# A graph network kernel whose head is issued in written order, with a product and the seen edges' sums moved

## The chip, the cores and the metric

The kernel runs on one core of one Trainium2 chip. The core has TensorE (PE), VectorE (DVE), ScalarE (ACT), GpSimd (POOL) and SyncE (SP), the last of which only issues DMAs here. The metric is the device time of one execution in microseconds, and the time of a kernel is the median of several executions. Everything is in float32 unless said otherwise.

## The reference

12500 nodes with 256 features, 200000 edges from `src` to `dst`, sorted by `dst`. Each edge has a weight.

```python
h = relu(layernorm(x))
e = h @ W_P + W_P_b + W_pos                       # 256 -> 128
for q, k, v, s, b in two_layers:                  # 8 heads of 16
    att = exp(clip(sum_per_head((e @ q)[src] * (e @ k)[dst]), -10, 10))
    att = att / (segment_sum(att, src)[src] + 1e-8)
    e = layernorm(segment_sum(att * (e @ v)[dst], src) + e) * s + b
x = x + e @ inv_w + inv_b                         # 128 -> 256
h = relu(layernorm(x))
out = x + segment_sum(edge_weight * (h @ w_nbr)[src], dst) + h @ w_own + bias
```

## The kernel before

Nodes are cut into 98 tiles of 128 (`NT`, the last one with 84 rows). Edges stand in columns of 128; gathers fetch one row per edge, 128 rows to a gather, from tables in HBM by indirect DMAs that POOL issues (L802).

**The head.** `sort_edges` sorts 256K packed keys by bitonic compares on DVE. A level has stages across columns (L543) and stages of its own (`stage`, L302 to L325: one minimum, L310, and one maximum, L312, each 128x1024), with `turned` (L327) transposing 128x128 blocks on PE and copying them back on ACT. There are 143 wide minima; 128 belong to the levels' `own` list, the others to the across parts and the last stage. `columns_out` writes the sorted columns. At the same time `embed` (L745 to L774) makes the embedding of a pair of tiles: statistics on DVE (L754, L755), the root on ACT (L758), scales on DVE (L759, L760), normalisation on ACT (L762), transposes on PE (L765), relu (L767), the product with `W_P` (L770, L771), a copy (L773), and `project`: transposes (L707), a copy (L709), the product with q, k and v (L718), copies (L719, L721) and stores to the table `tkv`. `plan_as_they_come` (L591) plans the third pass. The head's code (L1505 to L1543) writes these one after the other, and the framework's planner orders them by its costs. Two POOL memsets, of part of `q` and of all of `acc`, stand at the start. `general` is the flag that chooses between this short arm and a general one.

**Attention, layers 0 and 1** (`short_attention`, L1069). 163 steps of 8 gathered columns each ("far" edges). Their order is written out: the loop at L1265 to L1303 names what each engine does in a step, and works for nodes and for "seen" edges (edges whose other end is in the same or a neighbouring tile, handled without gathers) hang in slots, each with a step and a place in it (`put`, `other_work`). `seen(t, t0)` (L1085) registers a tile's loads at step t0 - 5, its main works at t0 - 3 to t0 - 1, and the addition at t0. `t0` is the step by which the tile's far edges are complete (`ends_by`). Then the node's after-works: `next_layer` (L972) in layer 0, `neighbour_rows` (L998) in layer 1. The latter ends with x + e @ inv_w (L1012, L1013), stored to `res_d`, a layernorm, transposes (L1042), a relu into `ht`, and `both` (L1047): two 512-wide products of `ht` with `w_nbr` and `w_own` side by side (L1051) plus the bias row (L1053). `rows` copies the first half for the store to the table `th`, and the own half into `q` and `acc` (L1059), which are the third pass's two accumulators (`acc1`).

**The third pass** (`short_neighbours`, L1306). 196 steps of 8 gathers from `th` (L802) into `kvg` (three buffers). In a step t: loads, `gathers(t + 2)` on POOL, `edge_hot(t + 1)` on DVE (L1343, ten selections into `hot`, two buffers), `adds(t - 1)` on DVE (L813), the results due, registers, and `sums(t)` on PE (L1356, L1358). `load_own` reads a tile's `res_d` three steps before its result; `result` (L1374) adds the accumulators to it and stores the output. The last step has three results due.

Of the kernel before, what the change touches and what calls it, by code (L numbers as in the profile page):

```python
# [37 lines left out]
P = 128  # L38
# [76 lines left out]
def gnn_kernel(ctx, tc, x, src, dst, edge_weight, wp_w, wp_b, w_pos, q1, k1, v1, ln1_s, ln1_b,  # L115
# [22 lines left out]
    bad = const.tile([P, 9], F32, name="bad")  # L138
# [61 lines left out]
    res_d = dram.tile([NT * P, GD], F32, name="res")  # L200
    place_d = dram.tile([P, W], BF16, name="place_d")
# [140 lines left out]
    def columns_out(pool, psum, a, b, c):  # L342
# [50 lines left out]
        fits = c[0:1, STEPS * (STEP + 2):STEPS * (STEP + 3)]  # L393
        nc.vector.tensor_tensor(fits, t8[:, STEP::STEP], firsts, op=OP.subtract)
        nc.vector.tensor_scalar(fits, fits, 1.0, None, op0=OP.is_gt)
        nc.vector.tensor_reduce(bad[0:1, 1:2], fits, AX.X, OP.max)
# [3 lines left out]
        nc.vector.tensor_tensor(bad[0:1, 1:2], bad[0:1, 1:2], fits[:, 0:1], op=OP.add)  # L400
# [29 lines left out]
    def sort_edges(pool, psum, mine, other, weight=None, idx=None):  # L430
# [87 lines left out]
        a, b = flipped(a, b, turn[:, 0:1])  # L518
        yield
        for level in range(1, LEVELS + 1):  # L520
            if level > LG and w is not None:
                bit = level - LG - 1
                a, b = flipped(a, b, turn[:, bit:bit + 1] if level == LEVELS else turn[:, 8 + bit:9 + bit])
                yield
                yield from turned(psum, a, b)
                a, b = b, a
                yield from turned(psum, w, w)
                for j in range(bit, -1, -1):
                    yield from stage(pool, a, b, w, LEVELS, j)
                    a, b = b, a  # L530
                yield from turned(psum, a, b)
                a, b = b, a
                yield from turned(psum, w, w)
            elif level > LG:
                yield from across(psum, a, b, level)
                if (level - LG) % 2:
                    a, b = b, a

                half = W // 4
                for c in (0, half):  # L540
                    lo, hi = (t[:, c:c + half] for t in (a, a[:, W // 2:]))
                    for op, t in ((OP.min, b), (OP.max, b[:, W // 2:])):
                        nc.vector.tensor_tensor(t[:, c:c + half], lo, hi, op=op)  # L543
                        yield
                a, b = b, a
            own = list(range(min(level, LG) - 1, -1, -1))
            if w is None:

                own = own[level > LG:len(own) - (level >= LG)]
            for j in own:  # L550
                yield from stage(pool, a, b, w, level, j)
                a, b = b, a
# [39 lines left out]
    def plan_as_they_come(pool, psum):  # L592
# [18 lines left out]
        room = pool.tile([P, NG, P], F32, name="room")  # L611
        nc.vector.tensor_tensor(room, d[:, :, 0:P], d[:, :, 1:], op=OP.is_gt)
# [17 lines left out]
        nc.scalar.copy(rows, pe[:NG])  # L630
        first, final = (rows[:, i, :].rearrange("g (w k) -> g w k", k=K) for i in range(2))
# [113 lines left out]
    def embed(node, psum, wp_sb, zb3, ones_b, q, tiles):  # L745

        n, many = rows_of(tiles[0]), len(tiles)
        mv = node.tile([P, 2, 2], F32, name="mv2", bufs=3)
        xts = []
        for i, t in enumerate(tiles):  # L750
            xt = node.tile([P, GD], F32, name="xt", bufs=5)
            nc.sync.dma_start(xt[:n], x[t * P:t * P + n, :])
            st = node.tile([P, 6], F32, name="st")
            nc.vector.bn_stats(st[:n], xt[:n])  # L754
            nc.vector.bn_aggr(mv[:n, i, :], st[:n])  # L755
            xts.append(xt)
        mean, dev = mv[:n, 0:many, 0], mv[:n, 0:many, 1]
        nc.scalar.activation(dev, dev, AF.Sqrt, bias=eps5[:n])  # L758
        nc.vector.reciprocal(dev, dev)  # L759
        nc.vector.scalar_tensor_tensor(mean, mean, -1.0, dev, op0=OP.mult, op1=OP.mult)  # L760
        for i, (t, xt) in enumerate(zip(tiles, xts)):
            nc.scalar.activation(xt[:n], xt[:n], AF.Identity, bias=mv[:n, i, 0:1], scale=mv[:n, i, 1:2])  # L762
            pt = psum.tile([P, 2, P], F32, name="pt", bufs=2)
            for k in range(2):
                nc.tensor.transpose(pt[:, k, :n], xt[:n, k * P:(k + 1) * P], ident[:n, :n])  # L765
            ht = node.tile([P, 2, P], F32, name="ht")
            nc.scalar.activation(ht[:, :, :n], pt[:, :, :n], AF.Relu)  # L767
            pz = psum.tile([P, 2 * GD], F32, name="pz")
            for k in range(2):
                nc.tensor.matmul(pz[:n, 0:D], ht[:, k, :n], wp_sb[:, k, :], start=(k == 0), stop=False)  # L770
            nc.tensor.matmul(pz[:n, 0:D], ones_b[:, :n], zb3, start=False, stop=True)  # L771
            e = node.tile([P, D], F32, name="e", bufs=4)
            nc.scalar.copy(e[:n], pz[:n, 0:D])  # L773
            project(node, psum, q, t, 0, e)  # L774
# [223 lines left out]
    def neighbour_rows(node, slots, weights, acc, acc1, t0, t):  # L998

        n = rows_of(t)  # L1000
        inv_sb, w2_sb = weights
# [42 lines left out]
        def relu():  # L1044
            ht = tiles["ht"] = node.tile([P, 2, P], F32, name="ht", bufs=1)
            nc.scalar.activation(ht[:, :, :n], tiles["pt2"][:, 0:2, :n], AF.Relu)

        def both():
            pz = tiles["pz"] = slots["psum"].tile([P, 4 * P], F32, name="out_c", tag="n2")
            for k in range(2):  # L1050
                nc.tensor.matmul(pz[:n], tiles["ht"][:, k, :n], w2_sb[:, k].rearrange("p a b -> p (a b)"),  # L1051
                                 start=(k == 0), stop=False)
            nc.tensor.matmul(pz[:n, GD:], ones_b[:, :n], rows3[:, 1, :], start=False, stop=True)  # L1053

        def rows():
            h = tiles["h"] = node.tile([P, GD], F32, name="out_rows")
            nc.scalar.copy(h[:n], tiles["pz"][:n, 0:GD])
            for h, to in enumerate(acc1):
                nc.scalar.copy(to[:n, t, :], tiles["pz"][:n, GD + h * D:GD + (h + 1) * D])  # L1059

        def store():
# [5 lines left out]
            (t3, "pe_out", both), (t3 + 1, "act_out", rows), (t3 + 1, "store", store))  # L1067

    def short_attention(wide, pool, psum, still, q, acc, layer, after, early=None):  # L1069
# [92 lines left out]
        before = -1  # L1162
        for t in range(NT):
            before = max(before + 1, (ends_by(t) - 1) // STEP + 1)
            seen(t, before)
# [140 lines left out]
    def short_neighbours(wide, pool, psum, acc1, plan):  # L1306
# [63 lines left out]
        def load_own(t):  # L1370
            xt = of["xt", t] = pool.tile([P, GD], F32, name="xt", bufs=6)
            nc.sync.dma_start(xt[:rows_of(t)], res_d[t * P:t * P + rows_of(t), :])

        def result(t):  # L1374
            n, xt = rows_of(t), of.pop(("xt", t))
            for h, to in enumerate(acc1):
                half = slice(h * D, (h + 1) * D)
                nc.vector.tensor_add(xt[:n, half], to[:n, t, :], xt[:n, half])
# [7 lines left out]
        for t in range(-4, steps + 1):  # L1386
            if t % 2 == 0:
                do(load, t // 2 + 2, steps // 2)
            for i in outs.get(t + 3 if t + 3 < steps else -1, ()):
                load_own(i)  # L1390
            if t == steps - 1:
                for i in outs[steps]:
                    load_own(i)
# [13 lines left out]
        for i in outs[steps]:  # L1407
            result(i)

    def short_arm(q, acc, acc1):  # L1410
        with tc.tile_pool(name="short", bufs=1) as wide, tc.tile_pool(name="short_p", bufs=1, space=PSUM) as psum, \
# [4 lines left out]
            with tc.tile_pool(name="short_a", bufs=1) as pool, tc.tile_pool(name="short_n", bufs=2) as node:  # L1416
                inv_sb = pool.tile([P, GD], F32, name="inv_sb")
                w2_sb = pool.tile([P, 2, 2, GD], F32, name="w2_sb")

                def load_weights():  # L1420
                    layer_rows(pool, True)
                    nc.sync.dma_start(inv_sb, inv_w)
                    for j, w in enumerate((w_nbr, w_own)):
                        nc.sync.dma_start(w2_sb[:, :, j, :], w.rearrange("(k p) n -> p k n", p=P))

                weights = (inv_sb, w2_sb)
# [4 lines left out]
            with tc.tile_pool(name="short_b", bufs=1) as pool:  # L1431
# [3 lines left out]
                short_neighbours(wide, pool, psum, acc1, plan)  # L1435
# [63 lines left out]
    nc.gpsimd.memset(acc.rearrange("p a b -> p (a b)"), 0.0)  # L1499
# [5 lines left out]
    with tc.tile_pool(name="sort_a", bufs=1) as sp, tc.tile_pool(name="node_a", bufs=2) as node, \  # L1505
            tc.tile_pool(name="come", bufs=1) as cp, tc.tile_pool(name="head", bufs=1) as hp, tc.tile_pool(name="spsum", bufs=2, space=PSUM) as spsum, \
            tc.tile_pool(name="npsum", bufs=1, space=PSUM) as npsum, \
            tc.tile_pool(name="cpsum", bufs=1, space=PSUM) as cpsum:
        for _ in sort_edges(sp, spsum, src, dst):
            pass  # L1510
# [5 lines left out]
        part = hp.tile([2, GD], BF16, name="part")  # L1516
        zb3 = hp.tile([3, D], BF16, name="zb3")
        row_of = lambda t: bass.AP(tensor=t.tensor, offset=t.offset, ap=[[0, 1], [1, t.shape[-1]]])
        nc.scalar.dma_start(left[0:1, 0:D], row_of(wp_b))
        nc.scalar.dma_start(left[0:1, D:], row_of(w_pos))  # L1520
        nc.vector.tensor_add(left[0:1, 0:D], left[0:1, 0:D], left[0:1, D:])
        for i in range(3):
            nc.vector.tensor_copy(part[0:1, 0:D], left[0:1, 0:D])
            nc.vector.tensor_sub(left[0:1, 0:D], left[0:1, 0:D], part[0:1, 0:D])
            nc.scalar.dma_start(zb3[i:i + 1], part[0:1, 0:D])
        for i, b in enumerate((inv_b, bias)):
            nc.scalar.dma_start(left[i:i + 1], row_of(b))
        for i in range(3):
            nc.vector.tensor_copy(part, left)
            nc.vector.tensor_sub(left, left, part)  # L1530
            for j in range(2):
                nc.scalar.dma_start(rows3[i:i + 1, j, :], part[j:j + 1])
        for t in range(0, NT - 2, 2):
            embed(node, npsum, wp_sb, zb3, ones_b, q, (t, t + 1))
        for t in range(NT - NT % 2 - 2, NT):
            embed(node, npsum, wp_sb, zb3, ones_b, q, (t,))
        for _ in plan_as_they_come(cp, cpsum):
            pass
        pb = cpsum.tile([P, 9], F32, name="pb", tag="turned")
# [40 lines left out]
```

## Time and profile before

| | us |
|---|---|
| median of 7 runs | 7353.97 (7348.05 to 7371.37) |
| profiled execution, its own time | 7359.23 |
| its span | 7357.4 |
| head: to the general flag / first layer work | 642.7 / 647 |
| layer 0, mean step | 12.89 |
| layer 1, mean step | 13.66 |
| third pass, from / mean step | 5089 / 11.5 |
| mean granted PE clock | 0.801 |

The profile is of one execution. Its span runs from the first to the last instruction on the core. Lines like `L310 DVE TENSOR_TENSOR keys<-keys 128x1024 f32<-128x1024 f32 x143 | 172.2, 1204 | 0.6` name a source line, engine, operation, the tiles written and read with partitions by elements, and how often; then busy us in all, mean ns of one, and idle us of the engine just ahead of them with what ended it. Lines with `<-` and three numbers are waits: us in total, times, the longest. "remote" stands for a releaser that the profile can't name, "issue" for time in which the engine waited for nothing that it shows. Shares of the chain of waits are shares of the time followed back from the end of a window.

### The profile page before, as it was taken

Reading aid. Unit: us, or ns where it says so; the run is one execution under the profiler, and the core shown is the slowest. Engines: PE = TensorE matmul, PEld = TensorE weight load, DVE = VectorE, ACT = ScalarE, POOL = GpSimd, SP = SyncE. Lnnn points to the kernel's source line nnn. Section 1 sums busy time; section 2 is a strip of 40 time slices with the busy share of each in tenths; the row PEclk is TensorE's granted clock in tenths of the full one; section 3 lists DMA queues with packets and bytes.
Section 4 is the critical chain, followed back from the end, with each engine's and each line's share of the span. In section 5 each row is a group of like instructions: output and inputs, shape, how many; then the busy total and the mean of one; then the engine's idle time right before and its main releaser. Section 6 shows DMA issues by size and latency. Waiting matters only on the chain.

```text
span 7357.4 us, 91646 instructions
## 1 busy us (share of the span) xinstructions
PE 4990.7 (68%) x26262; PEld 4121.1 (56%) x26262; DVE 4094.8 (56%) x9525; ACT 2690.1 (37%) x4814; POOL 3990.1 (54%) x4189
## 2 busy tenths in 40 slices
PE   6773777777776776777778777877555555555555
PEld 3443666666666665666666666664444444444444
DVE  8776666666666665666666666664333333333333
ACT  3442555555555554555555555553000000000000
POOL 0002555555555554555555555554666666666666
PEclk7666888888888887889988888888777777777777
DMA  3112444444444443444444444443333333333333
GB/s 97 57 58 75 125 130 128 129 126 130 129 128 128 131 124 114 130 129 128 128 133 128 126 134 127 127 130 98 90 95 97 97 101 104 102 107 110 107 113 111
DMA packets 536717, 839.01 MB, mean 114 GB/s; under 512 B 105934, under 2 KB 360093, under 8 KB 536235
## 3 DMA queue, kind: packets, MB, share of 16 engines
q0 software_dynamic: 200448, 547.62, 25.1%
q1 hardware_dynamic: 334617, 284.29, 13.6%
q8 instruction: 245, 4.01, 0.2%
q14 instruction: 237, 1.94, 0.1%
q10 hardware_dynamic: 1170, 1.15, 0.1%
HBM read 752.73 MB, written 79.91 MB: 113 GB/s over the span
## 4 chain that ended last, share of the span: by engine, by line
PE 35%; issue 16%; POOL 15%; DVE 15%; another core or an unknown queue 11%; ACT 4%; DMA 3%; DVEq 1%; SPq 0%; ACTq 0%; POOLq 0%
POOL kvg L802 15%; PE qe L1205 7%; PE ps L1244 6%; PE qe L1122 4%; DVE att L1217 3%; DMA kvg<-tkv,idx_a 2%; PE out_c L1051 2%; PE qe L1153 2%; DVE kvg L1215 2%; PE ps L1356 2%; PE pq L718 2%; PE qe L1207 1%; DVE hot L1343 1%; PE pz L770 1%
## 5 line engine op out<-in xcount | busy, mean ns | idle before, releaser
L802 POOL DMA_INDIRECT kvg<-tkv,idx_a x2608 | 2474.8, 949 | 2542.1 <-issue 1309.5
L802 POOL DMA_INDIRECT kvg<-th,idx_a x1568 | 1502.2, 958 | 813.7 <-issue 450.0
L1356 PE MATMUL ps<-kvg,hot 128*128 128x256 f32 x3136 | 1049.2, 483 | 981.6 <-issue 898.4
L1356 PEld LDWEIGHTS ps<-kvg,hot 128*128 128x128 f32 x3136 | 759.7, 248 | 1203.7 <-issue 1027.8
L1343 DVE TENSOR_SCALAR hot<-iota_f,place_a,plan 128x128 f32<-128x128 f32 x1960 | 521.4, 360 | 1433.8 <-remote 1245.4
L1244 PE MATMUL ps<-kvg,hot 128*128 128x136 f32 x5216 | 844.7, 309 | 347.4 <-issue 322.0
L1215 DVE TENSOR_TENSOR kvg<-qe,kvg 128x512 f32<-128x512 f32 x652 | 431.6, 687 | 1103.0 <-remote 373.7
L1244 PEld LDWEIGHTS ps<-kvg,hot 128*128 128x128 f32 x5216 | 750.2, 212 | 437.3 <-issue 377.6
L1205 PE MATMUL qe<-q,hot_t 128*128 x5216 | 845.6, 314 | 138.9 <-issue 42.1
L1205 PEld LDWEIGHTS qe<-q,hot_t 128*128 128x128 f32 x5216 | 768.2, 226 | 181.4 <-issue 77.4
L1122 PE MATMUL qe<-kvn,hot_s 128*128 128x128 f32 x4720 | 693.2, 299 | 93.4 <-issue 92.5
L1122 PEld LDWEIGHTS qe<-kvn,hot_s 128*128 128x128 f32 x4720 | 649.9, 215 | 106.4 <-issue 105.6
L1186 ACT ACTIVATE far<-spread,part_neg 128x1280 bf16<-128x1280 bf16 x326 | 446.4, 1369 | 19.6 <-DMA spread<-place_d 9.1
L1190 ACT ACTIVATE hot_t<-far,ones 128x1280 f32<-128x1280 bf16 x326 | 444.9, 1365 | 0.5
L1229 DVE TENSOR_TENSOR hot<-still,place_a 128x1152 f32<-128x1152 f32 x326 | 439.1, 1347 | 0.0
L1153 PE MATMUL qe<-rows_s,hot_e 128*128 128x136 f32 x1176 | 232.1, 346 | 299.4 <-DVE rows_s L1145 215.6
L1234 DVE TENSOR_TENSOR kvg<-still,kvg 128x1024 f32<-128x1024 f32 x326 | 394.9, 1211 | 22.6 <-ACT kvg L1223 16.2
L1217 DVE TENSOR_REDUCE att<-kvg 128x64 f32<-128x1024 f32 x326 | 397.7, 1220 | 11.2
L1153 PEld LDWEIGHTS qe<-rows_s,hot_e 128*128 128x128 f32 x1176 | 193.4, 238 | 341.5 <-issue 259.9
L813 DVE TENSOR_TENSOR acc<-acc,ps 128x256 f32 (+1 forms) x718 | 304.2, 424 | 122.1 <-PE ps L1246 49.0
L1102 ACT ACTIVATE far<-seen,part_neg 128x256 bf16<-128x256 bf16 (+1 forms) x588 | 337.8, 639 | 0.7
L1358 PE MATMUL ps<-kvg,hot 128*128 x784 | 296.6, 464 | 45.2 <-issue 44.2
(253 smaller groups left out, 6512.1 us busy)
## 6 DMA issues: line engine op xcount, KB each, us to landing
spread<-place_d SPq DMA_DIRECT2D x326, 256.0 KB
kvg<-tkv,idx_a POOLq DMA_INDIRECT x2608
kvg<-th,idx_a POOLq DMA_INDIRECT x1568
xt<-in_x_dram SPq DMA_DIRECT2D x194, 128.0 KB
spread<-ext_d SPq DMA_DIRECT2D x326, 64.0 KB
seen<-place_d SPq DMA_DIRECT2D x196, 96.0 KB
seen<-other SPq DMA_DIRECT2D x196, 96.0 KB
emb<-e SPq DMA_DIRECT2D x194, 64.0 KB
```

The costliest lines, as they stand in the source:

```text
L802: nc.gpsimd.indirect_dma_start(out=dest, out_offset=None, in_=table, in_offset=bass.IndirectOffsetOnAxis(ap=idx, axis=0))
L1122: nc.tensor.matmul(to[:, k, :], hot_t[:, at, :], kvn[:, b, half], start=(i == 0), stop=(i == len(have) - 1))
L1153: nc.tensor.matmul(out_of, its["hot"][:, k, :], its["rows"][:, k, :], start=(k == 0), stop=(k == SEEN - 1))
L1186: nc.scalar.activation(far, of.pop(("spread", i)), AF.Abs, bias=part_neg[:, 1:2])
L1190: nc.scalar.activation(hot_t.rearrange("p k e -> p (k e)"), of.pop(("far", i)), AF.Relu, bias=ones[:, 0:1], scale=-1.0)
L1205: nc.tensor.matmul(qe[:, k, :], hot_t[:, h * K + k, :], q[:, bass.ds(tiles[h * K + k], 1), :], start=(k == 0), stop=False)
L1215: nc.vector.tensor_mul(kk, qe, kk)
L1217: nc.vector.tensor_reduce(att, kvg[:, :, 0:D].rearrange("p k (h d) -> p k h d", d=HD), AX.X, OP.add)
L1229: nc.vector.tensor_tensor(hot, iota_p[:, None, :].to_broadcast([P, STEP + 1, P]), place_a[:, c:c + STEP + 1, None].to_broadcast([P, STEP + ...
L1244: nc.tensor.matmul(ps[:, bass.ds(at, 1), :].rearrange("p a b -> p (a b)") if k else ps[:, 0, :], of["hot", i][:, k, :], of["kvg", i][:, k, ...
L1343: nc.vector.tensor_scalar(hot[:, k, :], iota_f, plan[1][:, c:c + 1], plan[2][:, c:c + 1], op0=OP.is_equal, op1=OP.mult)
L1356: nc.tensor.matmul(ps[:, bass.ds(at, 1), :].rearrange("p a b -> p (a b)") if k else ps[:, 0, :], hot[:, w * K + k, :], hg[:, k, :], start= ...
```

## The change

It has three parts.

1. **The head in written order.** The framework's planner is switched off for the head. The sort yields after each minimum and each maximum of an `own` stage; after every second of these one slot of other work is issued. `embed` no longer issues anything itself; it returns nine works for a pair of tiles, which are given to the slots 3g - 3 (load), 3g, 3g + 1, ... 3g + 7 for the g-th group. There are 50 groups (48 pairs and the two last tiles), so slots run from -3 to 154. Seven slots are issued ahead of the compares, 128 within them, the rest after the sort. A pair has one load, one relu, one `e` copy and one store of `e`. The memset of `acc` moves behind the first own stage; the planning's pieces are issued every sixth slot from 30 on, the biases' at slots 20 and 40, with three `part` tiles for one. A minimum over a row of 1305 elements and a column of `bad` are added.

2. **The own-node product in the third pass.** In layer 1 `both` keeps only the product with `w_nbr` (two 256-wide matmuls); `ht` is stored to HBM (128 KB a tile), and `q` and `acc` are set to zero. In the third pass `load_own` reads `res_d` and `ht` four steps ahead, and a new `own(t)` on PE adds up `ht` @ `w_own`, `res_d`'s rows through the identity, and the bias row in PSUM, after the sums of the step before the result. `result` adds PSUM and accumulator.

3. **Seen edges three steps sooner.** Each tile's seen works hang three steps earlier than its far edges are complete (one tile to a step at most); the after-works stay.

```diff
@@ sort_edges
             for j in own:
-                yield from stage(pool, a, b, w, level, j)
+                for _ in stage(pool, a, b, w, level, j):
+                    yield "own"
                 a, b = b, a
@@ columns_out
+        nc.vector.tensor_scalar(t8, t8, float(NT), None, op0=OP.min)
...
@@ embed
+        def root():
+            nc.scalar.activation(of["dev"], of["dev"], AF.Sqrt, bias=eps5[:n])
+
+        def scales():
+            mean, dev = of["mean"], of["dev"]
+            nc.vector.reciprocal(dev, dev)
+            nc.vector.scalar_tensor_tensor(mean, mean, -1.0, dev, op0=OP.mult, op1=OP.mult)
...
+        def second():
+            et = node.tile([P, 2, P], F32, name="et", bufs=1)
+            nc.scalar.copy(et[:, 0:many, :n], of["pt"][:, 0:many, 0, :n])
+            of["pq"] = [psum.tile([P, 3 * D], F32, name="pq", bufs=2) for _ in tiles]
+            for i, pq in enumerate(of["pq"]):
+                nc.tensor.matmul(pq[:n], et[:, i, :n], qkv_sb[0].rearrange("p a b -> p (a b)"), start=True, stop=True)
...
+        return load, stats, root, scales, normal, first, embeds, second, results_of
@@ neighbour_rows
         def both():
+            nc.sync.dma_start(ht_d[t][:, :, :n], tiles["ht"][:, :, :n])
             pz = tiles["pz"] = slots["psum"].tile([P, 4 * P], F32, name="out_c", tag="n2")
             for k in range(2):
-                nc.tensor.matmul(pz[:n], tiles["ht"][:, k, :n], w2_sb[:, k].rearrange("p a b -> p (a b)"),
-                                 start=(k == 0), stop=False)
-            nc.tensor.matmul(pz[:n, GD:], ones_b[:, :n], rows3[:, 1, :], start=False, stop=True)
+                nc.tensor.matmul(pz[:n, 0:GD], tiles["ht"][:, k, :n], w_sb[:, k], start=(k == 0), stop=(k == 1))
...
-            for h, to in enumerate(acc1):
-                nc.scalar.copy(to[:n, t, :], tiles["pz"][:n, GD + h * D:GD + (h + 1) * D])
+        def nothing():
+            for to in acc1:
+                nc.vector.memset(to[:, t, :], 0.0)
@@ short_attention
-        before = -1
+        before, at = -1, 0
         for t in range(NT):
             before = max(before + 1, (ends_by(t) - 1) // STEP + 1)
-            seen(t, before)
+            at = max(at + 1, before - 3)
+            seen(t, at)
             after(slots, before, t)
@@ short_neighbours
+            ht = of["ht", t] = pool.tile([P, 2, P], F32, name="ht", bufs=7)
+            nc.sync.dma_start(ht[:, :, :n], ht_d[t][:, :, :n])
+
+        def own(t):
+            n, ht = rows_of(t), of.pop(("ht", t))
+            po = of["own", t] = psum.tile([P, 4 * P], F32, name="own", tag=f"n{1 + t % 2}")
+            for k in range(2):
+                nc.tensor.matmul(po[:n, 0:GD], ht[:, k, :n], own_sb[:, k], start=(k == 0), stop=False)
+            nc.tensor.matmul(po[:n, 0:GD], ident[:n, :n], of["xt", t][:n], start=False, stop=False)
+            nc.tensor.matmul(po[:n, 0:GD], ones_b[:, :n], rows3[:, 1, :], start=False, stop=True)
...
-                nc.vector.tensor_add(xt[:n, half], to[:n, t, :], xt[:n, half])
+                nc.vector.tensor_add(xt[:n, half], po[:n, half], to[:n, t, :])
...
             do(sums, t)
-        for i in outs[steps]:
+            for i in outs.get(t + 1, ())[:2]:
+                own(i)
+        for k, i in enumerate(outs[steps]):
             result(i)
+            for j in outs[steps][k + 2:k + 3]:
+                own(j)
@@ the head
-    nc.gpsimd.memset(acc.rearrange("p a b -> p (a b)"), 0.0)
...
-            tc.tile_pool(name="cpsum", bufs=1, space=PSUM) as cpsum:
-        for _ in sort_edges(sp, spsum, src, dst):
-            pass
+            tc.tile_pool(name="cpsum", bufs=1, space=PSUM) as cpsum, tc.manual_schedule():
...
+        when = (-3, 0, 1, 2, 3, 4, 5, 6, 7)
+        emit = {}
+        for g, tiles in enumerate(groups):
+            works = embed(node, npsum, wp_sb, zb3, ones_b, q, tiles)
+            for at, work in zip(when, works):
+                emit.setdefault(3 * g + at, []).append((-at, work))
...
+        own = 0
+        for kind in sort:
+            if kind == "own":
+                if own == 0:
+                    nc.gpsimd.memset(acc.rearrange("p a b -> p (a b)"), 0.0)
+                own += 1
+                if own % 2 == 0:
+                    next_slot()
+        while emit:
+            next_slot()
+        for _ in plan:
+            pass
```

## The prediction

> **What bounds the kernel now.** I read the engines and the granted clock of the whole, then 200 us windows inside each stage, then in each stage the waits, the chain of waits and the groups of instructions. Totals first: no engine is full, TensorE (PE) comes nearest.
>
> ```profile
> PE 4990.7 (68%) x26262; PEld 4121.1 (56%) x26262; DVE 4094.8 (56%) x9525; ACT 2690.1 (37%) x4814; POOL 3990.1 (54%) x4189
> PEclk7666888888888887889988888888777777777777
> ```
>
> Windows: length, then busy us of PE, PEld, DVE, ACT, POOL, then clock, DMA share, GB/s. They are one of the head (0 to 647), of attention layer 0 (to 2791), of layer 1 (to 5089) and of the third pass (to the end).
>
> ```profile
> 200.00:400.00 200.00, 143.71 (x448) 84.95 (x448) 156.74 (x291) 86.11 (x254) 0.00 (x0) 0.59 0.18 58
> 1400.00:1600.00 200.00, 146.49 (x957) 134.56 (x956) 127.63 (x253) 108.53 (x172) 117.65 (x124) 0.85 0.44 127
> 4000.00:4200.00 200.00, 155.06 (x974) 128.71 (x973) 126.57 (x260) 115.80 (x208) 111.79 (x119) 0.91 0.44 126
> 5600.00:5800.00 200.00, 111.53 (x361) 85.69 (x361) 73.31 (x260) 0.00 (x0) 134.58 (x141) 0.72 0.33 98
> ```
>
> The head is VectorE (DVE) with PE close behind at a clock of 0.59; the layers are PE with something else nearly as long; in the third pass PE has 88 of 200 us free.
>
> **1. The head.** Its waits and groups:
>
> ```profile
> DVE mv L759 <- ACT mv L758: 67.0, 30, 3.0
> L312 DVE TENSOR_TENSOR keys<-keys 128x1024 f32<-128x1024 f32 x143 | 174.0, 1217 | 0.0
> L310 DVE TENSOR_TENSOR keys<-keys 128x1024 f32<-128x1024 f32 x143 | 172.2, 1204 | 0.6
> L718 PE MATMUL pq<-qkv,et 128*128 128x384 f32 x194 | 141.4, 826 | 15.7 <-ACT et L709 14.8
> ```
>
> Compares run from 49.1 to 616.2, 567 us. In the timeline a wide stage (L310 and L312) repeats every 2.40 us, a 256-wide compare every 0.34, one of L501 every 0.40, of L543 every 0.65: 143 x 2.40 + 168 x 0.34 + 28 x 0.40 + 28 x 0.65 = 430 us. The embedding's seven DVE operations take 1.05 us a pair by pitch, 50 us in all. So 87 us are stalls, 67 of them L759 waiting for ACT's root, which the new order puts a slot later.
>
> After: a slot every wide stage outside the across levels, three slots a pair, 128 slots. DVE needs 3 x 2.40 + 1.05 = 8.25 us a pair. PE and ACT strictly in turn need, at this clock, about 9.7 (0.4 copy, 3.3 for L718's four, 1.1 transposes, 0.6 relu, 2.6 for the L770 and L771 matmuls, 0.4 copy, 0.9 transposes, 0.4 handing over); overlapped, 7.4 (143.7 us of PE over 19.5 pairs). I take 8.7, between the DVE bound and the chain in turn: 42.7 pairs x 8.7 = 371. The rest of the sort is 15 wide stages, the narrow ones, L501 and L543, 122 together, and 16 of the 41 us that they now wait for column turns (L310 28, L543 13): 138. The sort starts 6 us sooner (the cast behind the 11.3 us memset no longer delays it): 43 + 371 + 138 = 552; the memset beside the first compares and the extra minimum (a 1305-wide one took 0.82) add 3, the columns' way out 30 as now (616.6 to 642.8, with what follows to 647). But slots reach 131 of 154, so 6.3 pairs are computed only after that, with nothing to hide them: 54 us at 8.5. Sum 639 against 642.7, where the general flag is out: **-4**. At 8.25 a pair and 48 us of rest it is -29, at 9.7 and 61 it is +46.
>
> The memset of `acc` leaves a place where a cast lay in its shade: L1523 took 5.67 us there and 0.20 later, while an addition, L1521, took 0.28 in it. Moved, it stands beside compares with two SBUF inputs, the addition's kind, so about 1 us; the cast's case, a stop of 11, is the upper end. GPSIMD Engine Reference of the Trainium skill, section Key points, says that GpSimd contends on shared SBUF interfaces with DVE instructions in a 2-port mode or with two SBUF inputs. That speaks against the move, would make it up to 11 us instead of 1, and the row of the addition is against it.
>
> **2. Seen edges three steps sooner.** Same works, other meetings. About 1.8 tiles leave each layer's last three steps for its start; regressed on step times, a tile in a step adds 2.5 to 3.7 us. That is 4.5 to 6.7 a layer if the start has room: **-8** for both. One tile in five may meet other work, 20 x 1.2 = 24 a layer; bounds -40 and +40.
>
> **3. Own-node product out of layer 1.** Groups of 2900 to 4900 and the chain there:
>
> ```profile
> L1051 PE MATMUL out_c<-w_sb,ht 128*128 128x512 f32 x340 | 176.0, 624 | 18.3 <-issue 16.6
> L1053 PE MATMUL out_c<-rows,ones_b 3*128 3x256 bf16 x85 | 23.9, 281 | 4.5 <-issue 3.9
> L1012 PE MATMUL out_e<-inv_sb,et 128*128 128x256 f32 x174 | 63.1, 430 | 19.9 <-issue 19.8
> L1059 ACT COPY acc<-out_c 128x128 f32<-128x128 f32 x85 | 24.0, 283 | 0.0
> L1059 ACT COPY q<-out_c 128x128 f32<-128x128 f32 x85 | 23.1, 271 | 0.0
> by line: issue 14.5%; PE qe L1205 12.3%; PE ps L1244 12.2%; PE qe L1122 7.6%; PE out_c L1051 7.4%; DVE att L1217 3.9%; another core or an unknown queue 3.6%; PE qe L1153 3.3%; POOL kvg L802 3.3%; DVE kvg L1215 2.9%; PE qe L1207 2.8%; PE out
> ```
>
> PE loses half of L1051 and L1053: 88 + 23.9 = 112 us over 85 tiles, 129 over 98. 148 of L1051's 176 us (7.4% of 2000) lie on the chain, 0.84 of it: 129 x 0.84 = 108 is the most. How much other waits take back, layer 0 tells: its step is 12.89 us against 13.66, with 9.44 us of PE (146.49/200) against 10.59. Brought to one clock (x 0.85/0.91) layer 0 has 8.82, so 1.77 more PE made 0.77 more time, 0.43: 129 x 0.43 = 56. ACT's two copies, 54 us over 98 tiles, are mostly hidden at 115.80 of 200. I take **-60**, by layer 0, as it is the same loop; bounds -108 and 0. Added: two memsets of `acc` and `q` (L133's 128x128 one took 0.17 us, so 33 us over 98 tiles, DVE busy 63%) and a 128 KB store of `ht`. The store sits on SP's queue waiting for the relu, ahead of later `spread` and `seen` loads, which are issued steps early. **+2**; +33 if the memsets had no cover.
>
> TensorE: Matmul & The Clock Gate of the Trainium skill, section What's actually happening, has a clock of half speed after an idle window of about 3.4 us and full after a busy one. So taking PE work away can slow the rest. The rows agree in direction, 0.85 in layer 0 against 0.91. At 0.85 the 10.59 - 0.79 us of a step would grow by 0.7 and the gain be nearly gone; the factor from layer 0 already holds this loss.
>
> **4. Own-node product into the third pass.** There the gathers lead:
>
> ```profile
> L802 POOL DMA_INDIRECT kvg<-th,idx_a x1391 | 1332.9, 958 | 667.6 <-issue 400.3 <-remote 245.2 <-PE ps L1358 21.7
> L1356 PE MATMUL ps<-kvg,hot 128*128 128x256 f32 x2783 | 927.9, 482 | 862.3 <-issue 829.1 <-DMA kvg<-th,idx_a 24.4 <-DVE q L813 5.1
> DVE hot L1343 <- remote: 1091.4, 98, 17.2
> POOL kvg L802 <- remote: 245.2, 77, 4.6
> ```
>
> Eight gathers need 8 x (0.95 + 0.30) = 10.0 us; steps repeat as 12.4, 12.2, 10.0, mean 11.5. In the timeline POOL's late starts (6106.19, 6118.41) and DVE's (6105.96, 6118.18) come 0.8 us after the last landing of the step before (6105.2, 6117.4): sums end with the landings, then free the buffers. A tile adds six f32 instructions of 0.43 to 0.48 (L1012, L1356) and one bias row of 0.28: 3.0 us, 98 times, 295 us of PE, issued after a step's sums have freed the buffers. Next landings are 2.4 us off, and PE has some 5 us of the step free to catch up by the last. Its two loads go out four steps ahead on SP, behind the stores of results; own-to-result adds wait behind 3.6 us of `hot`. So nearly all is hidden: **+10**, bounds -20 (a clock above 0.72) and +200 (two of three steps wait: 65 x 3.0).
>
> **5. The end.** Tile 97's product waits for tile 95's result, then its own addition and store: **+2**.
>
> **Sum:** -4 - 8 - 60 + 2 + 10 + 2 = -58 on the profiled 7357.4 us span: 7299. That execution took 7359.2, 5.3 above the median of 7354.0, so a median near 7296.
>
> **Rivals.**
> A. *Larger gain:* DVE alone bounds the head (-29), layer 1 gives its chain share (-108), 3 to 5 as above: 7354 - 29 - 8 - 108 + 2 + 10 + 2 = 7223. For it: 0.84 of L1051 on the chain. Against: POOL waited 264.9 us there for PE's L1246 and 184.4 for L1042, waits that a free PE only moves. 0.12.
> B. *Slower by the third pass:* the release of `kvg` and `hot` comes behind the own product, so POOL starts late in each step with a tile. It decides once more than 0.7 us a tile shows, 68/98 of the gain elsewhere; 65 x 3.0 = 195 less 68 is 7481, half of it 7384. For: 245.2 us of POOL waits end with PE's sums. Against: own stands after the sums. 0.20.
> C. *Slower by the head:* PE and ACT in turn, 9.7 a pair, +46, and layer 1 only -20: 7354 + 46 - 8 - 20 + 14 = 7386. For: PE at half clock. Against: three pairs are in flight. 0.12.
> D. *Nothing comes of it:* gather and issue waits (14.5% of the chain) take layer 1's gain, the rest cancels: 7350. 0.08.
>
> My forecast has 0.48, alone 7240 to 7335. 0.2%, 15 us, is about what can be told from no change: faster 0.12 + 0.45 = 0.57, same 0.03 + 0.07 = 0.10, slower 0.33. The range, 7220 to 7450, leaves out the upper part of B and the low part of A.
>
> **What would show it.** Head: pairs every 8.3 to 9 us, L759's wait gone, 50 to 60 us of embedding after the last compare. Layer 1: steps of 13.3, L1051 at about 0.43 us each; clock below 0.9 would eat it. Third pass: steps still 11.5 with PE near 125 of 200 us; POOL kvg waits unchanged. Steps of 12.5 there, or a first gather after 660, make the prediction wrong.

## The result

| | us | ratio to before |
|---|---|---|
| before, 43 runs | 7358.1 (7337.35 to 7384.98) | |
| after, 17 runs | 7383.46 (7371.93 to 7399.6) | 1.0034, 95% interval 1.0026 to 1.0041 |
| after, the profiled execution | 7365.5 (span 7363.7) | |

The change makes the kernel 25 us slower; 58 us faster was forecast. The profiled execution was quicker than any of the 17 runs, so its stages account for 6 of the 25 us only; a second profile of the same kernel stands below.

One thing about the experiments first. They ran on six occasions, and the kernel before takes 7358, 7236 and 7224 us on three of them (granted clock 0.80, "slower chips" below) and 6050 to 6053 on the three others (0.89, "the faster chip"). These are names only: that it is the chip that differs is not shown, as the record numbers the chips of five occasions, and number 2 stands beside 6051 us and, 37 minutes later, beside 7224. Times are compared with the "before" of the same occasion; where stages of two occasions stand side by side, the text says so.

The profile after, engines and clock of the whole, then windows as shown of before (length, busy us of PE, PEld, DVE, ACT, POOL, clock, DMA share, GB/s):

```profile
PE 5008.7 (68%) x26850; PEld 4230.5 (57%) x26850; DVE 4127.4 (56%) x9721; ACT 2624.9 (36%) x4470; POOL 3976.1 (54%) x4189
PEclk7666888888888887899888888888777777777777
```

```profile
200.00:400.00 200.00, 137.00 (x495) 87.78 (x495) 191.55 (x335) 80.44 (x212) 0.00 (x0) 0.64 0.21 64
1400.00:1600.00 200.00, 141.28 (x931) 128.51 (x931) 128.28 (x259) 105.04 (x167) 116.58 (x124) 0.86 0.45 126
4000.00:4200.00 200.00, 146.89 (x945) 132.35 (x944) 124.92 (x276) 107.81 (x181) 108.03 (x114) 0.89 0.45 131
5600.00:5800.00 200.00, 110.49 (x381) 85.42 (x382) 73.35 (x260) 0.00 (x0) 134.06 (x142) 0.74 0.35 101
```

In the head DVE is now full, 191.55 of 200 us against 156.74. In layer 1 PE lost 8 us of 200, and the steps did not get shorter. The stages, taken from the traces (head: to the first L1217 reduction; layers: first to last of these; turns: what lies between two stages; third pass: first to last gather; end: from there):

| us | head | layer 0 | turn | layer 1 | turn | third pass | end |
|---|---|---|---|---|---|---|---|
| before | 683.7 | 2088.9 | 57.6 | 2213.3 | 51.4 | 2250.5 | 12.0 |
| after | 667.4 | 2094.6 | 61.5 | 2225.1 | 35.4 | 2256.2 | 23.5 |

The head gains 16 us, and the turn to the third pass 16 more; both layers, the third pass and the end each give some back. The groups of the head and, from 2900 to 4900, of layer 1 (count, busy us and mean ns, idle ahead):

```profile
L313 DVE TENSOR_TENSOR keys<-keys 128x1024 f32<-128x1024 f32 x143 | 174.1, 1218 | 0.0
L311 DVE TENSOR_TENSOR keys<-keys 128x1024 f32<-128x1024 f32 x143 | 173.6, 1214 | 2.2
L807 PE MATMUL pq<-qkv,et 128*128 128x384 f32 x194 | 134.6, 845 | 28.6 <-ACT et L804 28.6
```

```profile
L1094 PE MATMUL out_c<-w_sb,ht 128*128 128x256 f32 x340 | 94.2, 388 | 22.2 <-issue 21.8
L1102 DVE MEMSET q<- 128x128 f32 x85 | 14.0, 165 | 0.0
L1102 DVE MEMSET acc<- 128x128 f32 x85 | 14.0, 165 | 0.0
```

The product costs 94.2 us instead of 176.0 and 23.9, about as priced (88). Third pass, 5300 to 7300, groups and then the longest waits (us in total, times, longest):

```profile
L844 POOL DMA_INDIRECT kvg<-th,idx_a x1386 | 1315.8, 949 | 685.6 <-issue 393.3 <-remote 208.5 <-PE ps L1403 46.5
L1401 PE MATMUL ps<-kvg,hot 128*128 128x256 f32 x2768 | 857.0, 455 | 565.6 <-issue 456.8 <-DVE acc L855 53.5 <-DMA kvg<-th,idx_a 24.9
L1427 PE MATMUL own<-own_sb,ht 128*128 128x256 f32 x360 | 121.8, 461 | 33.6 <-issue 31.5 <-PE ps L1403 0.8
```

```profile
DVE hot L1388 <- remote: 945.1, 77, 14.8
POOL kvg L844 <- remote: 208.5, 66, 4.7
```

PE's idle time ahead of the first group of sums fell from 862 to 566 us, which is where the own products went; POOL's idle time is 686 against 668.

### The profile page after: what moved, and what is told of

It is laid out like the page before. It is cut to its first block, busy times and chain, and to the rows that moved or that the text cites. A ratio compares the mean times of both kernels' runs of the same rounds, so it can differ in the third digit from the quotient of the medians.

```text
span 7363.7 us, 92808 instructions
## 1 busy us (share of the span) xinstructions
PE 5008.7 (68%) x26850; PEld 4230.5 (57%) x26850; DVE 4127.4 (56%) x9721; ACT 2624.9 (36%) x4470; POOL 3976.1 (54%) x4189
## 5 line engine op out<-in xcount | busy, mean ns | idle before, releaser
L1401 PE MATMUL ps<-kvg,hot 128*128 128x256 f32 x3136 | 980.8, 458 | 669.6 <-issue 531.7
L1401 PEld LDWEIGHTS ps<-kvg,hot 128*128 128x128 f32 x3136 | 707.7, 232 | 880.0 <-issue 690.1
L1289 PE MATMUL ps<-kvg,hot 128*128 128x136 f32 x5216 | 880.9, 316 | 390.9 <-issue 367.3
L1289 PEld LDWEIGHTS ps<-kvg,hot 128*128 128x128 f32 x5216 | 783.7, 219 | 496.4 <-issue 441.7
L1151 ACT ACTIVATE hot_s<-far,ones 128x1280 f32<-128x1280 bf16 x196 | 267.2, 1363 | 233.0 <-remote 112.9
```

Source lines behind the costliest of these rows:

```text
L1289: nc.tensor.matmul(ps[:, bass.ds(at, 1), :].rearrange("p a b -> p (a b)") if k else ps[:, 0, :], of["hot", i][:, k, :], of["kvg", i][:, k, ...
L1401: nc.tensor.matmul(ps[:, bass.ds(at, 1), :].rearrange("p a b -> p (a b)") if k else ps[:, 0, :], hot[:, w * K + k, :], hg[:, k, :], start= ...
```

## The experiments

### The parts one by one, on a slower chip

Each is the kernel before with one part of the diff: the head; `at = max(at + 1, before - 3)` for the seen edges; the product moved; and head and product together.

> The kernel before with the head's part of the change alone. In the traces of before and after the first far gather goes out at 660.1 and 641.2 us of trace time, and the pairs of the embedding follow each other every 8.3 us. Both theories expect the head's gain to stay: 15 to 20 us less than before (7338 to 7343 against 7358), layers and third pass as before. If head work was only moved, the gain is gone by the end and the time is that of before within 5 us.

> The kernel before with the seen edges three steps sooner and nothing else. Theory A (the shift of the seen edges costs time in both layers, and hides in layer 1 what the moved product gains): 10 to 30 us slower than before, both layers longer. Theory B (layer 1 isn't set by PE, so that taking the product out gains nothing): within 5 us of before.

> The kernel before with the own-node product in the third pass and nothing else. Theory A: layer 1 gets 30 to 60 us shorter than its 2213, the third pass with its end some 15 us longer, so 15 to 45 us faster than before. Theory B: layer 1 within 10 us of 2213, the third pass and its end 15 to 20 us longer, so 5 to 30 us slower than before.

> The whole change without the shift of the seen edges. Theory A: 30 to 65 us faster than before, the sum of head and product. Theory B: the head's 15 to 20 us less and the product's 5 to 30 more, within 15 us of before. If the parts act on each other (a head that ends otherwise sets the layers' rhythm), the sum of the single parts misses this by over 10 us.

| before 7235.74 | median us | ratio, 95% |
|---|---|---|
| head | 7222.41 | 0.9978 (0.9969 to 0.9986) |
| seen edges three sooner | 7307.85 | 1.0096 (1.0080 to 1.0111) |
| product moved | 7217.96 | 0.9973 (0.9963 to 0.9984) |
| head and product | 7198.24 | 0.9941 (0.9925 to 0.9957) |

Theory A holds in its main point: the seen edges' shift alone costs 72 us, more than the other two gain, and more than the 10 to 30 that A expected. The single parts add up to +41 (-13 - 18 + 72); head and product together gain 38. Theory B falls, but A's 30 to 60 us from layer 1 were a little too many:

| us | head | layer 0 | turn | layer 1 | turn | third pass | end |
|---|---|---|---|---|---|---|---|
| head | 667.6 | 2044.9 | 58.2 | 2172.9 | 46.8 | 2231.0 | 13.8 |
| seen three sooner | 678.3 | 2062.9 | 62.2 | 2216.9 | 47.1 | 2231.9 | 13.7 |
| product moved | 677.0 | 2030.9 | 55.0 | 2145.3 | 38.5 | 2240.9 | 20.9 |
| head and product | 666.1 | 2035.4 | 55.4 | 2150.3 | 40.7 | 2240.2 | 22.8 |

The first row leaves layers and third pass as before, so it serves as their measure here. Each row is one profile: layer 0, which the moved product doesn't touch, is 14 us shorter in its row than in the first, so a layer's time is known to some 15 us only. The shift costs 18 us in layer 0, 4 at the turn and 44 in layer 1. The moved product gives 28 in layer 1 and 8 at the turn after it (46.8 to 38.5), and takes 10 in the third pass and 7 at the end: 19 in sum, beside the 18 of the medians.

### Why the shift costs

A tile comes about every five thirds of a step, so the seen works and a tile's first after-works repeat about every five steps. Theory M: seen works and after-works of tiles fall into the same step or not, depending on the shift modulo five. Theory N: being sooner is what costs. Shifts of two and of five, next to the kernel before again:

```diff
-            seen(t, before)
+            at = max(at + 1, before - 2)
+            seen(t, at)
```

> The kernel before itself, for a profile of it on the chip that runs the others of this call. Its stages, not its total, are wanted: layers near 2045 and 2173 us if the chip is like that of the runs with single parts, near 2089 and 2213 if it is like that of the first profile.

> The kernel before with the seen edges two steps sooner instead of three. Tiles come three to five steps. Counted by step modulo five, the seen edges' main PE work of a tile falls into a step with a tile's whole-row after-works in two of three tiles now, in three of three at a shift of three, in one of three at a shift of two. Theory M (what counts is which works meet in a step): not slower than before, 20 to 60 us faster. Theory N (being sooner is what costs, by longer lives of buffers or a crowded start): two thirds of the 72 us that three steps cost, 40 to 55 us slower.

> The kernel before with the seen edges five steps sooner, one whole period, so that the same works meet as before. Theory M: within 12 us of before. Theory N: 100 us slower or more.

They ran on the faster chip, and so shifts of two and three, and the whole change with a shift of two, were later put side by side, which came to the faster chip again:

> The kernel before with the seen edges two steps sooner. On a chip of the slower kind (kernel before above 7200 us): theory M (works that meet in a step) 20 to 70 us faster than before, theory N (being sooner costs) 40 to 55 us slower. On one of the faster kind (6050 us): 26 us faster, as in its first run.

> The kernel before with the seen edges three steps sooner, beside the shift of two on one chip. Slower kind of chip: 72 us slower than before, as in its first run, 90 to 140 above the shift of two by theory M, 20 to 30 by N. Faster kind: 25 to 50 us slower than before by M, 20 or less by N; the whole change there lost 45 us to the same change with a shift of two.

> The whole change with a shift of two. Slower kind of chip: by M the parts' sum, 13 + 18 us of head and product and 20 to 70 of the shift, so 50 to 100 us faster than before, where the whole change is 25 slower; by N 0 to 20 us slower. Faster kind: 95 us faster, as in its first run.

| faster chip, shift of | ratio, 95% | layer 1, mean step | turn after layer 0 |
|---|---|---|---|
| none (before 6050.4) | 1 | 10.52 | 38.2 |
| two | 0.9958 (0.9944 to 0.9971) | 10.27 | 48.4 |
| two again | 0.9964 (0.9951 to 0.9976) | 10.25 | 48.1 |
| three | 1.0078 (1.0063 to 1.0094) | 10.64 | 49.3 |
| five | 1.0049 (1.0035 to 1.0062) | 10.52 | 49.0 |

N falls: two steps sooner is faster, three slower, five has the steps of none. M holds for the steps and missed for five (28 us slower, 12 at most was expected; for three it was 53, with 25 to 50 expected): on this chip every shift makes the start of a layer longer, some 10 us at the turn and 8 to 22 ahead of layer 0 (660.2 without a shift, 667.9 to 681.7 with one; three more profiles with the same head and no shift have 653.5 to 664.3). That the first tiles' works now crowd the first steps is the likely reason, but no run singles it out. On the slower chip above, the start costs less: 4 us at the turn and 1 ahead of layer 0 (677.0 and 678.3). The whole change with a shift of two took 5957.79, 0.9849 (0.9835 to 0.9863).

What meets: layer 1's mean step by step number modulo five, steps 12 to 154, on the slower chips (the first two rows on one occasion, the whole change on another).

| step modulo 5 | 0 | 1 | 2 | 3 | 4 |
|---|---|---|---|---|---|
| no shift (head alone) | 13.44 | 13.26 | 13.89 | 13.25 | 13.63 |
| three (seen alone) | 13.37 | 13.80 | 13.08 | 13.66 | 14.97 |
| three (whole change) | 13.43 | 13.34 | 13.21 | 13.11 | 14.58 |
| two (whole change) | 13.94 | 13.21 | 13.17 | 13.26 | 12.90 |

With three, one step in five mostly holds a tile's main seen work, another's sums and a tile's whole-row after-works (counted from the loop, 19 of the 29 steps at 4; no step does with no shift or with two), and takes 14.6 to 15.0 us; the lighter steps don't give it back. PE is busy 12.55 us in these steps with the seen edges' shift alone, 10.94 with the head alone. 1.34 us more in some 32 steps make 43 of layer 1's 44 us.

On the faster chip other steps are the long ones, and what fits their times is the meeting of main seen work and whole-row after-works alone. Steps of layer 1 in which these two meet, by the same count, and the mean step there:

| step modulo 5 | 1 | 3 | 4 |
|---|---|---|---|
| no shift | 26 of 28, 11.69 | 7 of 29, 11.00 | 22 of 29, 10.94 |
| two | 7, 10.86 | none, 10.35 | 20, 10.85 |
| three | 28, 11.63 | 26, 11.98 | 21, 10.62 |

Down each column the time follows the count. The sums beside them, which mark the long steps on the slower chip (at 4), cost nothing here. So the steps' times follow the meetings on both, but which meeting costs most differs.

### Why layer 1 gained half of what was forecast

The product left out, with nothing in its place (no store of `ht`, no memsets), first by itself, then beside the moved one and the whole change:

```diff
-                nc.tensor.matmul(pz[:n], tiles["ht"][:, k, :n], w2_sb[:, k].rearrange("p a b -> p (a b)"),
-                                 start=(k == 0), stop=False)
-            nc.tensor.matmul(pz[:n, GD:], ones_b[:, :n], rows3[:, 1, :], start=False, stop=True)
+                nc.tensor.matmul(pz[:n, 0:GD], tiles["ht"][:, k, :n], w2_sb[:, k, 0], start=(k == 0), stop=(k == 1))
...
-            for h, to in enumerate(acc1):
-                nc.scalar.copy(to[:n, t, :], tiles["pz"][:n, GD + h * D:GD + (h + 1) * D])
```

> The kernel before without the own-node product in layer 1 and with nothing in its place: no store of ht, no memsets, the third pass as before (its sums start from what layer 1 left in q and acc, and the output lacks h @ w_own + bias). Layer 1 lost 28 us in the profile with the product moved. If the added store and memsets took back the rest, layer 1 is now 55 to 65 us shorter. If PE's work was worth only that much, because the clock falls as PE gets idle, layer 1 is 20 to 35 us shorter and the granted clock in it is 0.87 again, against 0.90.

> The whole change once more, for a profile on the chip of this call; the chips of the calls so far differ (the kernel before took 7358, 7236 and 6053 us on them). On a chip like the first two (granted clock 0.80): 15 to 45 us slower than before. On one like the third (0.89, where the layers' steps of 10.0 us are the eight gathers'): layer 0 within 10 us, layer 1 20 to 60 us shorter, the third pass 0 to 10 longer, so 10 to 60 us faster.

> The whole change with the seen edges two steps sooner instead of three. Theory M (works that meet in a step): 50 to 100 us less than the whole change at a clock of 0.80, 20 to 50 less at 0.89, and faster than before on either. Theory N: at most 25 us less than the whole change.

> The kernel before with the own-node product moved and nothing else, beside the one without that product. Third pass 5 to 12 us longer than before, its end 6 to 10. If the store of ht and the memsets cost the layers nothing, layer 1 is as short as in the kernel without the product, within 10 us; if they take back what was missing from the forecast, 25 us or more longer than that.

> Without the own-node product in layer 1 and with nothing in its place, third pass as before (the output lacks h @ w_own + bias and its sums start from what layer 1 left). At a clock of 0.80: layer 1 30 us shorter if PE's work is worth 28 us as in the profile with the product moved, 60 us if store and memsets took the rest. At 0.89: 80 us shorter, as in the first run of it.

| faster chip | ratio, 95% | layer 0 | layer 1 | third pass | end |
|---|---|---|---|---|---|
| before (6051.35; stages of the 6050.4 profile above) | 1 | 1620.4 | 1703.5 | 1967.2 | 13.2 |
| product left out, first time (beside 6053.19) | 0.9851 (0.9836 to 0.9866) | 1619.9 | 1620.0 | 1965.9 | 13.0 |
| product left out | 0.9843 (0.9830 to 0.9857) | 1621.5 | 1621.5 | 1965.3 | 12.8 |
| product moved | 0.9856 (0.9841 to 0.9872) | 1621.6 | 1623.2 | 1965.5 | 16.3 |
| whole change | 0.9916 (0.9903 to 0.9930) | 1626.8 | 1645.7 | 1968.3 | 17.3 |
| whole change, shift of two | 0.9843 (0.9830 to 0.9857) | 1617.2 | 1613.4 | 1964.3 | 17.0 |

Here layer 1 gains 80 us, until its step is 10.0 us, the eight gathers'; the first such run had been expected at 65 at most. Store and memsets cost no more than 2 us (1623.2 against 1621.5). In the third pass the moved product costs nothing, where 5 to 12 were expected, and 3 at the end. The whole change is 50 us **faster** on this chip. The last runs came to a slower chip (before 7224.34):

> The whole change with a shift of two, beside the whole change. On a chip of the slower kind (kernel before above 7200 us): 50 to 100 us faster than before if the parts add up there (13 + 18 + 20 to 70), within 20 us of before if the shift of two gains nothing there. On the faster kind: 95 us faster, as twice before.

> The whole change. Slower kind of chip: 15 to 45 us slower than before, so 70 to 130 above the shift of two. Faster kind: 50 us faster than before, 45 above the shift of two.

> Without the own-node product in layer 1 and with nothing in its place (the output lacks h @ w_own + bias and the third pass's sums start from what layer 1 left). Slower kind of chip: 25 to 45 us faster than before, with a lower clock and longer pauses ahead of PE's sums in layer 1, if it is PE's freed time that is given back there; 70 us or more if store and memsets took it. Faster kind: 95 us faster, as twice before.

| slower chip | median us | ratio, 95% | layer 0 | layer 1 |
|---|---|---|---|---|
| whole change, shift of two | 7200.62 | 0.9964 (0.9951 to 0.9977) | 2026.7 | 2144.0 |
| whole change | 7254.05 | 1.0041 (1.0028 to 1.0054) | 2044.5 | 2177.4 |
| product left out | 7199.60 | 0.9963 (0.9950 to 0.9976) | 2028.0 | 2149.9 |

The whole change is 30 us slower again, and 53 above its shift of two, where 70 to 130 were expected. M expected the shift of two to gain 20 to 70 us there by itself; 24 us of gain in all (17 to 35), where head and product alone reached 38 (31 to 54) on another occasion, say that it gains nothing. Whether it costs some 14 us stays open, as head and product alone did not run beside it. So on a slower chip a shift of two costs little or nothing and one of three costs much; that two helps is shown on the faster chip only. With the product left out and nothing added, the kernel is 25 us faster than its own before, and layer 1 only 23 us shorter than the 2172.9 of the head alone on the earlier occasion: the rest is given back by PE itself. Two views show it, head alone against product moved (same chip, 2900 to 4900): the window, and the group of the far edges' sums.

```profile
2900.00:4900.00 2000.00, 1606.51 (x9943) 1360.65 (x9942) 1267.98 (x2626) 1170.85 (x2062) 1119.05 (x1184) 0.90 0.46 132
```

```profile
L1285 PE MATMUL ps<-kvg,hot 128*128 128x136 f32 x2368 | 398.1, 316 | 148.4 <-issue 138.2 <-DMA kvg<-tkv,idx_a 8.9
```

Product moved:

```profile
2900.00:4900.00 2000.00, 1554.34 (x10012) 1410.04 (x10011) 1294.40 (x2839) 1157.62 (x1913) 1131.40 (x1197) 0.87 0.49 139
```

```profile
L1246 PE MATMUL ps<-kvg,hot 128*128 128x136 f32 x2400 | 419.3, 320 | 199.9 <-issue 185.6 <-DMA kvg<-tkv,idx_a 9.9 <-DVE hot_e L1138 1.2
```

By step (13.41 and 13.24 us): PE is busy 10.77 and 10.29 us, 0.48 less where 112 us over 85 tiles, 0.79 a step, were taken out; the clock fell from 0.90 to 0.87, and 10.0 us at 0.90 make 10.3 at 0.87. The pauses ahead of the sums grew from 1.00 to 1.32 us. So 0.79 taken out, less 0.31 and less 0.32, leaves 0.16, the 0.17 measured. The fit is closer than two profiles allow: their layer 0, which is the same code, differs by 0.08 us a step. The clock is the steadier part, 0.89 to 0.90 in the three profiles from slower chips that have the product in layer 1 and 0.87 to 0.88 in the six that don't; the pauses are 0.86 to 1.00 us a step with it and 0.96 to 1.32 without. On the faster chip the clock stays where it was, 0.97 with the product and 0.96 to 0.97 without (2400 to 3900).

## Why the prediction was wrong

- **Seen edges, -8 with bounds of 40 to either side: the step that failed.** Measured +72 alone, 80 us off and the largest miss of the sum; 53 from three to two within the whole change. The prediction spread the meetings evenly, "one tile in five", 1.2 us each; in fact the works repeat about every five steps, and a shift of three puts three of them into one, 1.34 us more in every fifth step of layer 1 and none of it given back elsewhere. It also counted on room at the layers' start, and the start got longer (the turn from 58.2 to 62.2 us). Its 2.5 to 3.7 us for a tile in a step is an estimate that no view here shows. No rival named this: both slower ones lay elsewhere.
- **Layer 1, -60: mechanism right, size off.** -28 on a slower chip, -80 on the faster one. The factor 0.43 from layer 0 stood at 28/129 = 0.22 where it was measured. TensorE: Matmul & The Clock Gate of the Trainium skill, section What's actually happening, has the clock halved after an idle window, and the fall from 0.90 to 0.87 agrees in direction; the prediction took the loss as held in its factor. The longer pauses it had not priced at all.
- **Third pass, +10: right,** 10 us on a slower chip (2231.0 to 2240.9), none on the faster one. The waits of POOL that rival B rests on went from 245.2 to 208.5 us and steps stayed at 11.5, so it is refuted; PE, from 5300 to 7100, went from 109 to 120 of 200 us, where near 125 was forecast. The turn ahead of it, 8 us shorter with the product moved, had no term.
- **The end, +2: 7 us** (13.8 to 20.9). After the last sums, at 7355.0 in the profile after, PE makes three tiles' products one by one until 7360.5, not one:

```profile
7355.41 1.03 PE L1427 MATMUL own<-own_sb,ht 128*128 128x256 f32 x4
7357.01 1.13 PE L1427 MATMUL own<-own_sb,ht 128*128 128x256 f32 x4
7358.71 1.09 PE L1427 MATMUL own<-own_sb,ht 128*84 128x256 f32 x4
```

- **The head, -4: -13,** within its bounds. Pairs follow every 8.3 us, the DVE bound and not 8.7; L759's successor, L774, waits 1.3 us among the compares, so the wait of 67.0 is gone there, and 40.1 us in the pairs after the sort, which nothing hides (the lines below: up to 565 us, then to 660). The columns' way out takes 27 us (542.6 to 569.2 in the timeline; 30 in the sum), and the pairs left over follow it and take 54 as forecast (570.6 to 624.2). What the sum had too long is the compares, which end at 542.6 and not at 555. Rival C is refuted.

```profile
DVE mv L774 <- ACT mv L770: 1.3, 4, 0.5
```

```profile
DVE mv L774 <- ACT mv L770: 40.1, 6, 7.6
```

- **The memset beside the compares costs nothing:**

```profile
43.55 11.33 POOL L1627 MEMSET acc<- 128x13464 f32 x1 [41.36 <-DVE keys L516]
```

```profile
45.92 1.23 DVE L311 TENSOR_TENSOR keys<-keys 128x1024 f32<-128x1024 f32 x1
56.73 1.22 DVE L311 TENSOR_TENSOR keys<-keys 128x1024 f32<-128x1024 f32 x1
```

A compare with two SBUF inputs takes 1.23 us inside the memset and 1.22 after it, against the contention that GPSIMD Engine Reference of the Trainium skill, section Key points, states for such instructions.

## What to carry to other kernels

Where an order is written out in slots, count for each slot of the period which works fall into it, before and after a shift, and price the fullest slot: the lighter ones don't pay it back. Work taken from an engine that is not alone in setting the pace is worth what the next wait leaves of it; look at the clock and the pauses of that engine first. A change in several parts is best measured part by part: here two good ones hid behind a bad one, and head and product without the shift took 0.9941 of the time on a slower chip, the whole with a shift of two 0.9964 on another slower one and 0.984 on the faster one.

## What the hardware showed unexpectedly

The same kernel took 7358 us on one occasion and 6050 on another. The group of the far edges' sums in layer 0 (900 to 2300) on the faster chip, then on a slower one:

```profile
L1244 PE MATMUL ps<-kvg,hot 128*128 128x136 f32 x2224 | 281.6, 280 | 0.8 <-PE out_e L985 0.8
```

```profile
L1244 PE MATMUL ps<-kvg,hot 128*128 128x136 f32 x1728 | 279.5, 306 | 135.2 <-issue 128.2 <-DMA kvg<-tkv,idx_a 5.5
```

The matmuls take 9% more; what differs most is pauses of PE ("issue") with no releaser in the trace. Work off PE takes the same on both: a gather 0.95 us, a layer's 128x1024 reduction 1.22. On the slower chips the matmuls that follow such pauses start at steps of about 0.70 us: of 344 pauses that the profile before puts down to "issue" from 700 to 2700 us, 127 end 0.6 to 0.8 us after the start of the matmul before, 114 at 1.3 to 1.6 and 27 at 2.0 to 2.4, with 47 between these; the faster chip has 35 in the same stretch of its trace, 32 of them at 0.6 to 0.8 and none from 1.3 up. In the third pass its steps follow each other every 10.04 us, about what eight gathers need, against 11.5. What makes the pauses stays open, and so does whether they belong to a chip or to an occasion; that they differ means that the sign of a change of 0.5% can differ too, as it did here.
